# Index lists of a graph network's gathers without a bound

## The chip, the cores and the metric

The kernel runs on one core of a Trainium2 chip. The metric is device time in microseconds (us), the median of several executions; a profile of one execution goes with it. In the profile PE is TensorE, PEld its weight load, DVE is VectorE, ACT is ScalarE, POOL is GpSimd, SP is the engine that issues plain transfers.

## The reference

Two layers of a relational graph attention network, a residual and a layer norm, on N = 3125 nodes with 768 features, E = 53,125 edges sorted by destination, and R = 3 relations. The first layer has 4 heads of 192, the second 1 head of 768.

```
def rgat_conv(x, W, q, k, b, src, dst, etype, heads, out_ch, n_nodes):
    xr = einsum('nd,rdf->rnf', x, W)          # a row for each node and relation
    oi = xr[etype, dst]; oj = xr[etype, src]
    alpha = leaky_relu(oi @ q + oj @ k, 0.2)
    m = segment_max(alpha, dst);  e = exp(alpha - m[dst])
    z = segment_sum(e, dst);      a = e / (z[dst] + 1e-16)
    msg = a[:, :, None] * oj.reshape(-1, heads, out_ch)
    return segment_sum(msg, dst) + b

h = elu(rgat_conv(x, W1, q1, k1, b1, ...))
out = layernorm(x + rgat_conv(h, W2, q2, k2, b2, ...))
```

## The kernel before

The nodes are taken in 25 groups (NB) of up to 128. The edges of a group are laid over 17 slots of 128 lanes (SL; 14 in group 0), a lane for an edge. Slots are whole, so some of their lanes hold edges of the next group, or, in the last group, lie behind the last edge. These lanes have a place `dl` in the group of 128 or more and never match a node.

For each slot the kernel gathers rows by an index list (`ridx`, 3 x source + relation), 128 indices for one instruction on POOL: `gather_rows`, L485. It does so from three tables in HBM of 9600 rows each (25 x 128 x 3; the rows of real nodes end at 3125 x 3 = 9375): `kt1`, the key products of layer 1, 16 bytes a row; `tab1`, the transformed rows of layer 1, 3088 bytes; `tab2`, those of layer 2, 3088 bytes. There are 24 x 17 + 14 = 422 slots, so 3 x 422 = 1266 gathers, all from the one line L490, and the profile tells them apart by their target: `kt`, `share` and `g` (tab1), `G` (tab2).

The stages follow each other in an order that is written out by hand (a list of steps for each count of products or gathers), with no reordering behind it:

- **0 to about 108 us**: preparation of the edges, key and query products.
- **Phase 1**, to about 770 us. For each group an index chain: a transpose into PSUM (`a_index`), then `a_index2` (L575) on DVE, which makes `dl` (L580), the index list, `rel` (L588) and a limit `lim` (L592); `a_next` and `a_next2` find where the next group begins. With the list there, the group's kt gathers are issued (for groups 0 to 20), and scores, a segmented maximum by scan and weights `pall` are made. Meanwhile TensorE makes the rows of tab1 from x (L742); every sixth of its matmuls waits for a gather that lies 8 earlier, as "an even load".
- **Loading of the second weights**, to about 820 us.
- **Phase 2**, to about 1756 us. The tab1 gathers go into 14 buffers (9 `share` and 5 `g`); per group the weighted sums are matmuls in two batches (L1028, 8 and 9 slots), and between these lie the matmuls of the second layer's rows (L1121). A gather waits for the sums of the slot 14 before. The kt gathers of the last four groups lie between, four to a group (`KEYS`), for groups 2 to 18.
- **Phase 3**, to the end. The tab2 gathers go into 44 buffers, with scores, scan, sums (L1340), layer norm and output beside them.

A gather of the kernel before carries a bound, 9599: a lane whose index is above it isn't transferred. `a_index2` adds 2^20 to the index of every lane outside its group (L584, L585), so that those lanes are dropped. A dropped lane leaves in its buffer what was there, so for groups 0 to 2, where a buffer has no rows yet, the index is limited to 9599 instead (`rfirst`, L587).

Of the kernel before, what the change touches and what calls it, by code (L numbers as in the profile page):

```python
# [8 lines left out]
F32 = mybir.dt.float32  # L9
# [3 lines left out]
I32 = mybir.dt.int32  # L13
AF = mybir.ActivationFunctionType
ALU = mybir.AluOpType
# [5 lines left out]
P = 128  # L21
# [11 lines left out]
def _index(ap):  # L33
    return bass.IndirectOffsetOnAxis(ap=ap, axis=0)
# [3 lines left out]
SL = 17  # L38
# [22 lines left out]
def kernel(  # L61
# [20 lines left out]
    N, D = x.shape  # L82
    R = layers[0]["W"].shape[0]
    E = src.shape[0]
    NB = (N + P - 1) // P
    NP = NB * P
# [11 lines left out]
    LL = FRONT + E + BACK  # L98
    NK = (NB - 1) * SL + SLF
    V, S, G, T = nc.vector, nc.scalar, nc.gpsimd, nc.tensor  # L100
    OOB = float(1 << 20)

    dram = ctx.enter_context(tc.tile_pool(name="fdram", bufs=1, space=DRAM))
    keep = ctx.enter_context(tc.tile_pool(name="keep", bufs=1))
    first_rows = {0: 0, 1: 1, 2: 2}

    ed_d = dram.tile([4, LL], F32, name="ed_d")
    dr_d = dram.tile([1, LL], BF, name="dr_d")
# [30 lines left out]
    oidx = keep.tile([P, 1], I32, name="oidx")  # L139
    flag = keep.tile([1, 1], I32, name="flag")  # L140
    ridx = keep.tile([P, NB, SL], I32, name="ridx")
    rfirst = keep.tile([P, len(first_rows), SL], I32, name="rfirst")
    dl = keep.tile([P, NB, SL + 1], F32, name="fdl")
    rel = keep.tile([P, NB, SL], F32, name="rel")
    pall = keep.tile([P, NB, SL, H1], F32, name="pall")
# [318 lines left out]
    def slots(b):  # L464
        return SL if b else SLF
# [18 lines left out]

    def gather_rows(to, tab, b, j):  # L485

        i = ridx[:, b]
        if b in first_rows:
            i = rfirst[:, first_rows[b]]
        return G.indirect_dma_start(out=to, out_offset=None, in_=tab, in_offset=_index(i[:, j:j + 1]),  # L490
                                    bounds_check=NP * R - 1, oob_is_err=False)

    def start(b, into):

# [56 lines left out]
    def phase1(pre, work, psum, wH, wL, qq):  # L551
# [23 lines left out]
        def a_index2(b):  # L575
            pT = st[b]["pi"]
            c = SL + 1

            p3 = pT[:SHIFT, :3 * c].rearrange("p (r k) -> p r k", r=3)
            V.tensor_copy(p3[:, :, 0], p3[:, :, slots(b)])  # L580
            V.tensor_scalar(dl[:, b, :], pT[:, c:2 * c], 1.0 / BIG, n_all[:, b:b + 1], op0=ALU.mult,
                            op1=ALU.subtract)
            inv = work.tile([P, SL], F32, name="inv", bufs=2)
            V.tensor_scalar(inv, dl[:, b, :SL], float(P), OOB, op0=ALU.is_ge, op1=ALU.mult)  # L584
            V.tensor_add(ridx[:, b, :], pT[:, 0:SL], inv)  # L585
            if b in first_rows:
                V.tensor_scalar(rfirst[:, first_rows[b], :], ridx[:, b, :], NP * R - 1, None, op0=ALU.min)  # L587
            V.tensor_copy(rel[:, b, :], pT[:, 2 * c:2 * c + SL])  # L588

            s = st[b]  # L590
            s["lim"] = work.tile([P, 1], F32, name="lim", bufs=2)
            V.tensor_scalar(s["lim"], n_all[:, b:b + 1], float(P), float(N), op0=ALU.add, op1=ALU.min)  # L592
# [39 lines left out]
        def a_gather(b, j):  # L632
            gathered[b, j] = gather_rows(kts[b % 3][:, j, :], kt1, b, j).ins
# [180 lines left out]
        for _ in range(4):  # L814
            T.matmul(ahead[0][:, :P], ident, ident, start=True, stop=True)
        d_split(1)
        a_index2(0)
        for j in range(SLF):
            a_gather(0, j)
# [28 lines left out]
        ev = {}  # L848

        chain = ((-6, a_index), (-6, a_index2), (-5, a_gathers), (-5, a_next), (-4, a_next2))  # L850
        turn = [base(b) * STEPS // NE for b in range(NB - LATE)]
        for b, n in enumerate((4, 3, 2, 1)):
# [39 lines left out]
        for n in range(max(ev) + 1):  # L892
            for f, b in ev.get(n, ()):
                f(b)
            b, i = divmod(n, 6)
# [37 lines left out]
    def phase2(work, psum, wH, wL):  # L933
# [19 lines left out]
        def key(b, j):  # L953
            gather_rows(kts[b % 2][:, j, :], kt1, b, j)
# [43 lines left out]
        def gather(k):  # L998
            gather_rows(gs[k % NG], tab1, *in_turn(k))
# [545 lines left out]
    with tc.manual_schedule():  # L1545
        with tc.tile_pool(name="share", bufs=1) as pool:
# [4 lines left out]
            with tc.tile_pool(name="wbuf", bufs=1) as wbuf:  # L1551
                wH = wbuf.tile([P, DT, WW], F32R, name="wH")
                wL = wbuf.tile([P, DT, WW], F32R, name="wL")
                with tc.tile_pool(name="pre", bufs=1) as pre:
                    qq = pre.tile([P, NB, H1, R], F32, name="qq")
                    with tc.tile_pool(name="work0", bufs=1) as work, tc.tile_pool(
                        name="psum0", bufs=1, space=PSUM
# [23 lines left out]
                    with tc.tile_pool(name="work1", bufs=1) as work, tc.tile_pool(  # L1581
                        name="psum1", bufs=1, space=PSUM
# [544 lines left out]
```

## Time and profile before

| what | us |
|---|---|
| runs | 2512.51, 2497.31, 2531.09 |
| median | 2512.51 |
| profiled execution | 2528.77 |
| its span | 2527.0 |
| PE busy | 1899.4 (75%) |
| POOL busy | 1332.5 (53%) |
| DVE busy | 1199.7 (47%) |
| mean granted clock of TensorE | 0.839 |
| bytes moved, all queues | 506.39 MB |

The span is that of the profiled execution, a little longer than the median run. "Busy" counts instructions at work. A row of instructions names line, engine, operation, output<-inputs, and in square brackets the idle time before it with what ended it. A windows row gives for a stretch of the span the busy time of each engine, the granted clock, the share of the DMA engines and GB/s.

### The profile page before, as it was taken

Reading aid. Unit: us, or ns where it says so; the run is one execution under the profiler, and the core shown is the slowest. Engines: PE = TensorE matmul, PEld = TensorE weight load, DVE = VectorE, ACT = ScalarE, POOL = GpSimd, SP = SyncE. Lnnn points to the kernel's source line nnn. Section 1 sums busy time; section 2 is a strip of 40 time slices with the busy share of each in tenths; the row PEclk is TensorE's granted clock in tenths of the full one; section 3 lists DMA queues with packets and bytes.
Section 4 is the critical chain, followed back from the end, with each engine's and each line's share of the span. In section 5 each row is a group of like instructions: output and inputs, shape, how many; then the busy total and the mean of one; then the engine's idle time right before and its main releaser. Section 6 shows DMA issues by size and latency. Waiting matters only on the chain.

```text
span 2527.0 us, 40133 instructions
## 1 busy us (share of the span) xinstructions
PE 1899.4 (75%) x13939; PEld 1335.0 (53%) x13939; DVE 1199.7 (47%) x4331; ACT 383.1 (15%) x834; POOL 1332.5 (53%) x1326
## 2 busy tenths in 40 slices
PE   8958987787689688889889889997445444465556
PEld 8746766576568466666666667766122222222223
DVE  7424434333344564555555656652254444445445
ACT  6301111111111011111111111111011111111111
POOL 4355666554350565555555565551656555556552
PEclk9978989898889789899999999999566666676667
DMA  7533444343338766666666768874777777777772
GB/s 228 146 112 112 150 146 149 102 144 113 119 110 307 248 214 206 212 197 211 217 202 213 223 206 253 252 229 169 254 237 269 256 265 239 236 239 246 239 243 102
DMA packets 161765, 506.39 MB, mean 200 GB/s; under 512 B 48027, under 2 KB 57520, under 8 KB 161555
## 3 DMA queue, kind: packets, MB, share of 16 engines
q0 software_dynamic: 81936, 331.52, 42.5%
q1 hardware_dynamic: 69389, 157.78, 17.8%
q10 hardware_dynamic: 10230, 14.43, 1.7%
q8 instruction: 114, 1.87, 0.3%
q14 instruction: 96, 0.79, 0.1%
HBM read 412.74 MB, written 95.69 MB: 201 GB/s over the span
## 4 chain that ended last, share of the span: by engine, by line
PE 51%; issue 20%; another core or an unknown queue 9%; POOL 8%; DVE 7%; DMA 2%; ACT 1%; POOLq 0%; DVEq 0%; SPq 0%; ACTq 0%
PE po L1121 17%; PE po L742 16%; PE acc L1028 9%; POOL G L490 7%; PE acc L1340 3%; DVE selp L482 2%; PE bank L299 1%; DMA G<-ftab,ridx 1%; PE pt L277 1%; PE pt L1095 1%; PE po L414 1%; PE px L714 1%; DVE sT L1251 0%; PE pq L649 0%
## 5 line engine op out<-in xcount | busy, mean ns | idle before, releaser
L490 POOL DMA_INDIRECT kt<-kt,ridx x374 | 393.8, 1053 | 260.6 <-DVE al L672 111.9
L490 POOL DMA_INDIRECT G<-ftab,ridx x374 | 378.2, 1011 | 273.4 <-PE acc L1340 118.2
L1121 PE MATMUL po<-wH,hT 128*128 128x512 f32 (+1 forms) x1500 | 449.9, 384 | 32.4 <-ACT r L1148 17.2
L742 PE MATMUL po<-wH,xT 128*128 128x512 f32 (+1 forms) x1320 | 431.6, 403 | 46.5 <-issue 34.3
L1340 PE MATMUL acc<-G,selp 128*32 128x384 f32 (+1 forms) x2292 | 303.8, 635 | 162.6 <-issue 88.9
L482 DVE TENSOR_SCALAR selp<-frow,fdl,pall 128x32 f32<-128x32 f32 (+1 forms) x1688 | 380.6, 316 | 31.7 <-remote 26.4
L490 POOL DMA_INDIRECT share<-ftab,ridx x239 | 239.9, 1004 | 206.1 <-PE acc L1028 125.4
L1121 PEld LDWEIGHTS po<-wH,hT 128*128 128x128 f32 x1500 | 274.4, 192 | 107.6 <-issue 37.4
L742 PEld LDWEIGHTS po<-wH,xT 128*128 128x128 f32 x1320 | 258.1, 204 | 103.4 <-issue 46.1
L1340 PEld LDWEIGHTS acc<-G,selp 128*32 128x32 f32 x2292 | 127.6, 133 | 312.5 <-issue 191.7
L1121 PE MATMUL po<-wL,hT 128*128 128x512 f32 (+1 forms) x750 | 285.4, 381 | 0.5 <-issue 0.2
L742 PE MATMUL po<-wL,xT 128*128 128x512 f32 (+1 forms) x660 | 261.2, 396 | 11.2 <-issue 10.1
L1028 PE MATMUL acc<-share,selp 128*32 128x193 f32 x3088 | 229.5, 363 | 46.0 <-issue 35.2
L490 POOL DMA_INDIRECT g<-ftab,ridx x135 | 136.0, 1007 | 129.0 <-PE acc L1028 79.5
L1028 PEld LDWEIGHTS acc<-share,selp 128*32 128x32 f32 x3088 | 144.0, 120 | 109.2 <-issue 87.3
L1148 ACT COPY r<-po 128x262 f32<-128x262 f32 (+5 forms) x175 | 71.2, 436 | 713.5 <-PE po L1121 348.4
L1121 PEld LDWEIGHTS po<-wL,hT 128*128 128x128 f32 x750 | 144.4, 193 | 28.4 <-issue 2.0
L742 PEld LDWEIGHTS po<-wL,xT 128*128 128x128 f32 x660 | 134.3, 203 | 39.3 <-issue 16.5
L1028 PE MATMUL acc<-g,selp 128*32 128x193 f32 x1688 | 134.3, 350 | 15.8 <-issue 15.1
L1251 DVE TENSOR_SCALAR sT<-bc,cols 128x512 bf16<-128x512 f32 (+1 forms) x125 | 82.8, 662 | 96.2 <-PE bc L1245 93.2
L1245 PE MATMUL bc<-d,one 1*128 1x512 bf16 (+1 forms) x125 | 48.8, 391 | 96.3 <-DVE sT L1251 65.1
L1028 PEld LDWEIGHTS acc<-g,selp 128*32 128x32 f32 x1688 | 82.6, 116 | 48.5 <-issue 38.6
(309 smaller groups left out, 1963.7 us busy)
## 6 DMA issues: line engine op xcount, KB each, us to landing
ftab<-r SPq DMA_DIRECT2D x74, 386.0 KB
ftab<-share SPq DMA_DIRECT2D x71, 386.0 KB
share<-in_L_gnn_W_dram SPq DMA_DIRECT2D x36, 384.0 KB
w_d<-w2hl SPq DMA_DIRECT2D x18, 768.0 KB
sT<-dr_d SPq DMA_DIRECT2D x25, 534.0 KB
share<-in_x_dram SPq DMA_DIRECT2D x27, 384.0 KB
xb_d<-share SPq DMA_DIRECT2D x25, 384.0 KB
xr<-in_x_dram SPq DMA_DIRECT2D x21, 384.0 KB
```

Of the source, the lines that this page charges most:

```text
L277: T.transpose(pt[:, f, c * P:(c + 1) * P], a[:, (2 * i + f) * P:(2 * i + f + 1) * P], ident)
L299: T.matmul(to, a[:, 2 * i + f, :], t[:, f, :w], start=(n == 0), stop=(n == 2 * DT - 1))
L414: T.matmul(po[g][:, :HALF], a[:, t % 2, :], w[:, t, KQ + r * D + c * HALF:][:, :HALF], start=(t == 0 and n == 0), stop=(t == DT - 1 and n ...
L482: V.tensor_scalar(sel.rearrange("p (t f) -> p t f", f=32), of, dl[:, b, j:j + 1], p, op0=ALU.is_equal, op1=ALU.mult)
L490: return G.indirect_dma_start(out=to, out_offset=None, in_=tab, in_offset=_index(i[:, j:j + 1]), bounds_check=NP * R - 1, oob_is_err=False)
L742: m = T.matmul(po[:, :n], xT[:, s, t, :], w[:, t, KQ + f:KQ + f + n], start=(i == 0), stop=(i == 3 * DT - 1))
L1028: T.matmul(acc[32 * t:32 * t + 32, h // 2, c], sel[:, h, 32 * WINDOW[i].index(t):][:, :32], g[:, h * CW:(h + 1) * CW], start=(i == u[0] an ...
L1121: T.matmul(po[:, :n], hT[:, k, t, :], w[:, t, f:f + n], start=(i == 0), stop=(i == 3 * DT - 1))
L1148: S.copy(o[:, 1 + at - a:1 + at + m], po[:, got - a:got + m])
L1245: T.matmul(bc[:, :n], one, s["d"][:, 4 * i * P:4 * i * P + n], start=True, stop=True)
L1251: V.tensor_scalar(s["sT"][:, 4 * i * P:4 * i * P + n], bc[:, :n], cols[:, b:b + 1], None, op0=ALU.is_equal)
L1340: T.matmul(acc[32 * t:32 * t + 32, c, :HALF + c], st[b, j][:, 32 * WINDOW[j].index(t):][:, :32], gs[:, (base(b) + j) % NG, 1 + c * HALF:][ ...
```

## The change

`gather_rows` passes neither a bound nor the flag that goes with it, and always takes `ridx`. `a_index2` doesn't mark the lanes outside their group any more: the index that stands at the lane, which is that of its own edge (of the next group) is limited to 0 and the last real row, 9374, in one instruction. With this every lane of every gather transfers a row. The marked sum, the first groups' own list and its tile go.

```diff
-    OOB = float(1 << 20)
-    first_rows = {0: 0, 1: 1, 2: 2}
...
-    rfirst = keep.tile([P, len(first_rows), SL], I32, name="rfirst")
...
     def gather_rows(to, tab, b, j):
 
-        i = ridx[:, b]
-        if b in first_rows:
-            i = rfirst[:, first_rows[b]]
-        return G.indirect_dma_start(out=to, out_offset=None, in_=tab, in_offset=_index(i[:, j:j + 1]),
-                                    bounds_check=NP * R - 1, oob_is_err=False)
+        return G.indirect_dma_start(out=to, out_offset=None, in_=tab, in_offset=_index(ridx[:, b, j:j + 1]))
...
-            inv = work.tile([P, SL], F32, name="inv", bufs=2)
-            V.tensor_scalar(inv, dl[:, b, :SL], float(P), OOB, op0=ALU.is_ge, op1=ALU.mult)
-            V.tensor_add(ridx[:, b, :], pT[:, 0:SL], inv)
-            if b in first_rows:
-                V.tensor_scalar(rfirst[:, first_rows[b], :], ridx[:, b, :], NP * R - 1, None, op0=ALU.min)
+            V.tensor_scalar(ridx[:, b, :], pT[:, 0:SL], 0.0, float(N * R - 1), op0=ALU.max, op1=ALU.min)
```

## The prediction

> **What bounds the kernel now.** I read the shares and the chain of the page first, then the windows stage by stage, then who waits for whom in each stage, and last the gathers themselves, since they are what the change touches.
>
> ```profile
> span 2527.0 us, 40133 instructions
> PE 1899.4 (75%) x13939; PEld 1335.0 (53%) x13939; DVE 1199.7 (47%) x4331; ACT 383.1 (15%) x834; POOL 1332.5 (53%) x1326
> PE 51%; issue 20%; another core or an unknown queue 9%; POOL 8%; DVE 7%; DMA 2%; ACT 1%; POOLq 0%; DVEq 0%; SPq 0%; ACTq 0%
> ```
>
> The chain that ended last is TensorE for half of the span. POOL, which issues the 1266 gathers, carries 8% of it. So a gather is not the pace of the kernel as a whole; what it is worth depends on the stage.
>
> ```profile
> 820.00:1000.00 180.00, 140.63 (x1190) 103.42 (x1194) 96.27 (x421) 16.09 (x33) 99.83 (x99) 0.84 0.71 226
> 1000.00:1250.00 250.00, 219.92 (x1910) 161.11 (x1906) 134.45 (x570) 29.62 (x60) 140.62 (x139) 0.93 0.66 207
> 1250.00:1490.00 240.00, 215.12 (x1885) 163.29 (x1881) 135.25 (x580) 28.60 (x60) 134.67 (x134) 0.93 0.69 215
> 1490.00:1755.00 265.00, 250.80 (x2254) 189.09 (x2243) 144.98 (x622) 37.77 (x79) 118.45 (x118) 1.00 0.70 222
> 1756.00:1815.00 59.00, 18.19 (x79) 5.46 (x79) 16.70 (x81) 1.59 (x2) 42.27 (x42) 0.53 0.85 287
> 1815.00:2485.00 670.00, 356.82 (x2747) 149.40 (x2746) 304.23 (x964) 88.20 (x111) 384.16 (x381) 0.66 0.73 244
> ```
>
> After the stretch's length the columns are the busy time of TensorE, its weight load, VectorE, ScalarE and POOL, then the granted clock, the DMA share and GB/s. The first four rows are phase 2, and its last one is close to a TensorE bound: 251 of 265 us busy at clock 1.00. The rows before it are not, and the waits name the difference:
>
> ```profile
> PE po L742 <- issue: 45.2, 52, 4.5
> PE acc L1028 <- issue: 44.8, 97, 1.1
> PE acc L1028 <- issue: 5.5, 21, 1.0
> PE acc L1340 <- issue: 88.9, 45, 7.4
> POOL kt L490 <- DVE al L672: 111.9, 9, 24.0
> POOL G L490 <- PE acc L1340: 129.4, 23, 8.7
> ```
>
> These are, in order, TensorE in phase 1 (110 to 760 us), in phase 2 before 1490, in phase 2 after 1490, and in phase 3, with the total, the times and the longest; then what POOL itself waited for in phases 1 and 3. In phase 1 POOL waits for VectorE to free a buffer, in phase 3 for TensorE to finish with one of 44: there the gathers run ahead. "issue" is a wait for nothing that the profile shows. Before 1490 the late 16-byte gathers (kt) lie among the others, four to a group; after it there are none, and the wait falls from 44.8 to 5.5 us. One such place, POOL first and TensorE below it:
>
> ```profile
> 1206.20 1.00 POOL L490 DMA_INDIRECT kt<-kt,ridx  x1 [0.30 <-issue]
> 1207.50 1.00 POOL L490 DMA_INDIRECT kt<-kt,ridx  x1 [0.30 <-issue]
> 1208.81 1.00 POOL L490 DMA_INDIRECT kt<-kt,ridx  x1 [0.30 <-issue]
> 1210.11 1.00 POOL L490 DMA_INDIRECT kt<-kt,ridx  x1 [0.30 <-issue]
> ...
> 1209.56 0.49 PE L1028 MATMUL acc<-share,selp 128*32 128x193 f32 x2 [0.94 <-issue]
> 1210.97 0.49 PE L1028 MATMUL acc<-share,selp 128*32 128x193 f32 x2 [0.92 <-issue]
> 1212.40 0.38 PE L1028 MATMUL acc<-g,selp 128*32 128x193 f32 x2 [0.95 <-issue]
> ```
>
> The sums step forward in pauses of 0.9 us while the four kt gathers are under way, and run freely behind them. I don't know what holds them; I take the pauses to last as long as the gathers do. A gather costs POOL 1.00 us and 0.30 us of "issue": a period of 1.30 us.
>
> **The change, part by part.**
>
> *The gather without a bound.* No row of this trace shows one. What there is:
>
> ```profile
> L490 POOLq MOVE  x1266: 29/29/29, 90.5 to 2480.0; - x181
> L490 POOL DMA_INDIRECT kt<-kt,ridx x374: 993/1000/1749, 190.7 to 1506.6; - x187
> L490 POOL DMA_INDIRECT kt<-kt,rfirst x48: 993/1000/1608, 108.3 to 186.2; - x48
> 68.47 0.73 POOL L397 DMA_DIRECT2D kt<-kk  x1 [3.18 <-DVE kk L396]
> 69.22 0.38 POOL L400 TENSOR_TENSOR qq<-g 128x12 f32<-128x12 f32 x2
> 2483.04 1.00 POOL L490 DMA_INDIRECT G<-ftab,ridx  x1 [0.30 <-issue]
> 2484.34 1.00 POOL L490 DMA_INDIRECT G<-ftab,ridx  x1 [0.30 <-issue]
> ```
>
> (Minimum, median and maximum in ns in the first three.) The 1266 moves that put the bound into a register go, 29 ns each. They lie on POOL's queue beside the gather before, so I cost them at nothing; without that cover it is 37 us over the run, 0.03 per gather. The check's own price can't be read off: gathers whose indices were clamped (rfirst) take 1.00 us, and so do the last two of all, whose every lane is past the bound. The work doesn't depend on the outcome of the check, which doesn't say that the check is free. From below, a plain DMA of 128 partitions, with no list and no bound, takes 0.73 us and the next instruction follows it with no pause: 0.57 under the period. From above, the slowest gather took 1.75 us: 0.75 over it. The nearest row is the gather with its bound. What it has and the plain one lacks is the pause of 0.30, which a list of indices, or an operand from a register, may cause; I take half of it, a saving of **0.15 us** (11.5% of 1.30), and keep both ends.
>
> What that is worth, stage by stage: the pauses of TensorE under kt gathers are 45.2 + 44.8 = 90 us, and 11.5% of them is 10.4. In phase 3 the 88.9 us lie partly in the first fill of 44 buffers, where the DMA share is 0.85 and the transfers set the landing, and for the rest in groups that POOL runs ahead of; I count half, 11.5% of 44 = 5.1. Elsewhere a quicker gather meets the buffers that POOL waits for already (the rows of 111.9 and 129.4) and waits longer: 0.
>
> *The index arithmetic.*
>
> ```profile
> L584 DVE TENSOR_SCALAR inv<-fdl x25: 176/177/178, 106.8 to 797.5; 128x17 f32<-128x17 f32 x25
> L585 DVE TENSOR_TENSOR ridx<-pT,inv x25: 175/176/178, 107.0 to 797.7; 128x17 int32<-128x17 f32 x25
> L587 DVE TENSOR_SCALAR rfirst<-ridx x3: 174/176/239, 107.2 to 163.9; 128x17 int32<-128x17 int32 x3
> POOL kt L490 <- DVE lim L592: 32.5, 5, 15.7
> ```
>
> 50 instructions of 0.18 become 25 of the same kind and shape, and the three minima go: 28 x 0.18 = 5.0 us of VectorE, which is 47% busy. On the path are only the places where POOL waits for the index list, five in phase 1 by the last row (it names the next instruction, lim): 5 x 0.18 = 0.9 us, say 1. Nothing else moves: on every engine the order of what stays is as before, SP's queue included, and no wait is added.
>
> *The rows that were skipped.* By the inputs, 768 of 54,016 lanes per table lie outside their group and past the clamped first groups; 370 of them are the end of the last group.
>
> ```profile
> DMA packets 161765, 506.39 MB, mean 200 GB/s; under 512 B 48027, under 2 KB 57520, under 8 KB 161555
> q0 software_dynamic: 81936, 331.52, 42.5%
> ```
>
> Now each fetches its row: 768 x 3088 bytes x 2 tables = 4.74 MB, 0.9% of 506.39 (the third table's rows have 16 bytes). At the 222 and 244 GB/s of the windows this is 2.37/0.222 + 2.37/0.244 = 20 us of transfer, but at a DMA share of 0.70 and 0.73, beside TensorE in phase 2 and 44 buffers in phase 3; that hides it, and I charge nothing. Without the cover it is the 20 us, half of it in the last group, where the last three gathers of each table become whole ones and the 370 lanes all read the last row.
>
> *Sum.* 10.4 + 5.1 + 1 = 16.5 us, so the profiled execution of 2528.77 us (span 2527.0) would be 2512. That execution is 16 us above the median of the three runs, 2512.51, from which I forecast **2496 us**, 0.7% less.
>
> **The rivals.**
>
> *A far cheaper gather that frees TensorE too.* The check and its register are the main part of what sets a gather apart, and it drops to the plain DMA's 0.73 us, 44% less. 44% of the 90 us is 40, of the 44 in phase 3 19. Then the clock: where pauses are rare (the window from 1490) 1.00 is granted, before it 0.84 and 0.93. At 1.00 the 576 us of TensorE there would be shorter by at most 9% (the mean before 1490 is 0.91), 54 us; half of it is 27. With the 1 us of indices this is 87: **2426 us**, and some 2450 with half of the clock's part. For it: the step from 44.8 to 5.5 us between neighbouring windows. Against: the list of 128 indices stays. The Trainium skill (TensorE: Matmul & The Clock Gate, Part 1) says that the clock falls to half after an idle window of about 3.4 us and is full again after a busy one; the windows agree in direction, and by that rule the clock's part comes all or nothing as pauses fall under one window.
>
> *The change does nothing to a gather.* Its time is that of making 128 descriptors, which stay 128. For it: the same 1.00 us for lists of every kind. Then only the 1 us of indices is left: **2511 us**. The Trainium skill (DMA: Bandwidth & Descriptors, the latency section) puts about 1 us on the emission of a DMA by the GpSimd path, whatever it moves, and names no bound; the trace's 1.00 us agrees, and by that rule the gather would stay as it is.
>
> *Slower: a gather without a bound takes POOL longer, and POOL becomes the pace.* A bound lets the lane be dropped; without one, another path of the same engine might be walked.
>
> ```profile
> L490 POOL DMA_INDIRECT G<-ftab,ridx x374: 994/1002/1429, 1834.1 to 2484.3; - x187
> ```
>
> In phase 3, 374 gathers take 650 us, 29.6 us for a group of 17. POOL's 17 x 1.30 = 22.1 fit in; from a period of 1.74 us they don't. A gather as slow as this row's slowest, 1.43 + 0.30 = 1.73, stands at that point: the pauses of 90 us grow by a third, +30, and phase 1, with bursts of 17, loses some 10 at its start. At 1.85 phase 3 adds 22 groups x 1.9 = 42. So +40 to +85, about **2575 us**. Against: no reason in the trace why less work should take longer.
>
> **How the numbers follow.** My forecast (saving 0 to 0.3 us per gather, 2480 to 2508) has 0.38; the far cheaper gather 0.30 (2400 to 2465); no effect 0.11 (2505 to 2520); slower 0.21 (2540 to 2610). The range, 2420 to 2585, leaves out a third of the cheap gather and nearly half of the slow one, 0.2 together; it takes in the 20 us of uncovered transfer. Two per cent, 50 us, is about what a measurement of this kernel can tell from no change: its three runs lie 34 us apart. Faster by more than that (under 2462): nearly all of the cheap gather and a little of mine, 0.31. Slower (over 2563): most of the last case, 0.19. Within: 0.50.
>
> **What would show it.** In the profile after, the gather's median and the pause before it in a burst: 0.85 to 1.0 us and 0.15 to 0.3 for my case. The rows "acc L1028 <- issue" and "po L742 <- issue" should lose about a tenth; if they fall by far more, or the clock before 1490 reaches 1.00, the first rival holds. Bytes of q0 rise by 4.7 MB, and no move stands before a gather. I am wrong if the pauses don't follow the gather's length at all (they may be made by the small rows, which stay), if the last group ends late behind its 370 equal rows, or if the gather's time leaves 0.7 to 1.3 us.

## The result, and the profile after

The changed kernel takes **2637.48 us** (median of 4 runs, 2622.75 to 2651.93) against 2521.8 for the kernel before: ratio **1.051**, 95% interval 1.044 to 1.057. It is slower, where 0.7% less was forecast. Five series of runs followed, each with its own runs of the kernel before on the same chip, and they fell into two kinds: in three of them the kernel before took 2512 to 2528 us again, in two it took 1944 and 1946. The results give no reason for the two kinds. The comparison above belongs to the first kind, which the text calls *held*; the second is called *free*. What separates them in the profile is the subject of this section and the next.

From the page of the changed kernel in the held series above: span, busy shares, packets, and the engines' shares of the chain that ended last.

```profile
span 2650.1 us, 38839 instructions
PE 1899.9 (72%) x13939; PEld 1344.5 (51%) x13939; DVE 1191.9 (45%) x4303; ACT 382.8 (14%) x834; POOL 1257.2 (47%) x1326
DMA packets 161755, 511.06 MB, mean 193 GB/s; under 512 B 47263, under 2 KB 56756, under 8 KB 161555
PE 33%; issue 17%; another core or an unknown queue 11%; POOL 11%; DVE 2%; DMA 2%; ACT 2%; SPq 0%; POOLq 0%; DVEq 0%; ACTq 0%
```

TensorE has the same work (1899.9 us against 1899.4) and VectorE and POOL have less. 4.67 MB more are moved. All the same the span is 123 us longer, so the time went into waiting. The gathers did get cheaper; by the view of their line in the changed kernel (L484; minimum, median and maximum in ns, then the first and last start):

```profile
L484 POOL DMA_INDIRECT kt<-kt,ridx x422: 938/944/1717, 107.7 to 1581.2; - x141
L484 POOL DMA_INDIRECT G<-ftab,ridx x422: 940/946/1380, 1837.6 to 2607.3; - x141
L484 POOL DMA_INDIRECT share<-ftab,ridx x272: 940/946/1258, 874.6 to 1783.1; - x136
```

0.946 us against 1.002, and with the pause of 0.30 a period (from the start of one gather to the start of the next) of 1.25 against 1.306. No move is left. The first starts date the loss: the first gather of tab1 stood at 825.1 and is now at 874.6 (+49.5 us in phase 1), the first of tab2 at 1760.2 and now 1837.6 (+27.9 in phase 2), and the remaining 45.7 us are phase 3. There it is spread over the groups: from one `oh` to the next, most groups take longer than before, by up to 6.6 us, and some are up to 3 us shorter. In a later held series the same changed kernel had its first tab1 gather at 869.3 and its first tab2 gather at 1796.6 us, in a span of 2611.0. So the loss of phases 1 and 3 came again (44 and 48 us), and that of phase 2 did not (927.3 us against 935.1 before).

The waits over the whole run, the kernel before first (VectorE, then TensorE) and the changed one below (its lines have other numbers: L1260 is L1271 of before, L1329 is L1340, L1017 is L1028, L731 is L742, L479 is L482):

```profile
DVE oh L1271 <- remote: 208.8, 24, 29.4
PE acc L1340 <- DVE selp L482: 66.7, 12, 8.9
PE acc L1028 <- issue: 50.3, 118, 1.1
```

```profile
DVE oh L1260 <- remote: 259.8, 24, 19.5
PE acc L1329 <- DVE selp L479: 185.2, 23, 9.1
PE acc L1017 <- issue: 66.2, 127, 1.6
PE po L731 <- issue: 57.7, 58, 3.0
```

The waits of TensorE for L742 stood in the prediction: 45.2 us. Every group of phase 3 but one has the wait in the first row. "remote" is the profile's word for a wait whose end it can put down to no instruction. The product `oh` on VectorE needs 17 small matmuls of TensorE (`pq`), and in the program it waits for nothing else on another engine. One group of the changed kernel, TensorE, VectorE and POOL from the timeline:

```profile
2007.55 0.62 PE L1254 MATMUL pq<-q2s,sT 128*128 128x9 bf16 x17
...
2018.95 0.32 DVE L1260 TENSOR_TENSOR oh<-oh,pq 128x153 f32<-128x153 f32 x1 [10.30 <-remote]
...
2016.32 0.95 POOL L484 DMA_INDIRECT G<-ftab,ridx  x1 [0.30 <-issue]
2017.58 0.95 POOL L484 DMA_INDIRECT G<-ftab,ridx  x1 [0.30 <-issue]
2021.42 0.94 POOL L484 DMA_INDIRECT G<-ftab,ridx  x1 [2.90 <-remote]
```

By the profile the 17 matmuls start within 0.62 us from 2007.55 on, and 16 matmuls of the sums follow them. Yet VectorE starts `oh` at 2018.95, when POOL's unbroken row of gathers has just ended. Counted from the start of the last of the 17 to the start of `oh`, the median of the 25 groups is 11.4 us here, 8.6 in the kernel before, and 0.57 in a free series; in the last group, with no gather left, it is 0.56 here too. While VectorE stands, the `selp` that it makes behind `oh` isn't there, and TensorE waits in turn: that is the second row. The profile models the ends of matmuls, so it can't say whether the work or the word of it is late.

The same is seen at the start of phase 1. These are the windows view, 108 to 130 and 130 to 150 us, for the kernel before and the changed one (columns as in the prediction: TensorE and its count first, the clock, the DMA share and GB/s last), and then single starts in the changed kernel: a matmul of the index chain and the instruction on VectorE that needs it, and a row of TensorE's products:

```profile
108.00:130.00 22.00, 18.22 (x88) 14.60 (x87) 6.05 (x23) 2.07 (x8) 16.75 (x17) 1.00 0.83 166
130.00:150.00 20.00, 2.61 (x8) 1.71 (x7) 0.00 (x0) 0.80 (x1) 14.39 (x15) 0.63 0.07 2
```

```profile
108.00:130.00 22.00, 19.40 (x87) 15.42 (x85) 5.14 (x21) 2.08 (x8) 16.82 (x18) 0.92 0.72 165
130.00:150.00 20.00, 3.16 (x9) 2.38 (x9) 0.00 (x0) 0.80 (x1) 12.54 (x14) 0.56 0.04 1
```

```profile
126.86 0.28 PE L587 MATMUL pT<-fdl,after 128*128 128x1 f32 x2
151.50 0.28 DVE L590 TENSOR_SCALAR n_all<-pT,n_all,lim 128x1 f32<-128x1 f32 x1 [27.46 <-remote]
...
133.90 0.37 PE L731 MATMUL po<-wH,xT 128*128 128x256 f32 x1 [1.83 <-issue]
136.00 0.37 PE L731 MATMUL po<-wH,xT 128*128 128x256 f32 x1 [1.73 <-issue]
137.40 0.37 PE L731 MATMUL po<-wL,xT 128*128 128x256 f32 x1 [1.03 <-issue]
140.20 0.38 PE L731 MATMUL po<-wH,xT 128*128 128x256 f32 x1 [2.42 <-issue]
143.00 0.37 PE L731 MATMUL po<-wH,xT 128*128 128x256 f32 x1 [2.42 <-issue]
```

VectorE starts 24.6 us after the matmul that it needs. Of TensorE's matmuls, eight or nine start in 20 us, and the starts shown lie 2.1, 1.4, 2.8 and 2.8 us apart: multiples of 0.70. This is the **hold**: beside a row of gathers TensorE makes one step at a time, or the word of its results comes late.

The hold doesn't set in with the first gather of a row. POOL's row began at about 108 us, and through its first 17 or 18 gathers, at the same period, TensorE nearly kept its pace (88 and 87 matmuls in 22 us); only behind them did it stop. Nor does the hold grow with the number of gathers under way. Counted from the DMA packets of the changed kernel's trace, 4 to 5 gathers were under way at each start from the 7th to the 16th, and 2 in the held part behind.

### The profile page after: what moved, and what is told of

It reads as the page before. It is cut to its first block, busy times and chain, and to the rows that moved or that the text cites. A ratio compares the mean times of both kernels' runs of the same rounds, so it can differ in the third digit from the quotient of the medians.

```text
span 2650.1 us, 38839 instructions
## 1 busy us (share of the span) xinstructions
PE 1899.9 (72%) x13939; PEld 1344.5 (51%) x13939; DVE 1191.9 (45%) x4303; ACT 382.8 (14%) x834; POOL 1257.2 (47%) x1326
## 4 chain that ended last, share of the span: by engine, by line
PE 33%; issue 17%; another core or an unknown queue 11%; POOL 11%; DVE 2%; DMA 2%; ACT 2%; SPq 0%; POOLq 0%; DVEq 0%; ACTq 0%
PE po L1110 15%; POOL G L484 11%; PE acc L1017 8%; PE po L731 6%; PE acc L1329 2%; DMA G<-ftab,ridx 1%; ACT r L1137 1%; PE pt L1084 0%; ACT ey L1036 0%; PE acc L1373 0%; ACT hT L1091 0%; DVE sT L1240 0%; DVE selp L479 0%; DMA ftab<-r 0%
## 5 line engine op out<-in xcount | busy, mean ns | idle before, releaser
L484 POOL DMA_INDIRECT G<-ftab,ridx x422 | 400.5, 949 | 423.7 <-PE acc L1329 170.3
L484 POOL DMA_INDIRECT kt<-kt,ridx x422 | 417.9, 990 | 379.4 <-DVE al L661 140.1
L731 PE MATMUL po<-wH,xT 128*128 128x512 f32 (+1 forms) x1320 | 437.6, 407 | 77.9 <-ACT share L763 39.3
L1110 PE MATMUL po<-wH,hT 128*128 128x512 f32 (+1 forms) x1500 | 457.9, 388 | 44.7 <-ACT r L1137 33.2
L1329 PE MATMUL acc<-G,selp 128*32 128x384 f32 (+1 forms) x2292 | 293.5, 639 | 210.7 <-DVE selp L479 185.2
L484 POOL DMA_INDIRECT share<-ftab,ridx x272 | 257.8, 948 | 354.9 <-PE acc L1017 185.7
L479 DVE TENSOR_SCALAR selp<-frow,fdl,pall 128x32 f32<-128x32 f32 (+1 forms) x1688 | 380.5, 325 | 26.1 <-remote 20.3
L731 PEld LDWEIGHTS po<-wH,xT 128*128 128x128 f32 x1320 | 261.8, 207 | 140.1 <-issue 50.6
L1329 PEld LDWEIGHTS acc<-G,selp 128*32 128x32 f32 x2292 | 131.7, 136 | 346.2 <-DVE selp L479 217.4
L731 PE MATMUL po<-wL,xT 128*128 128x512 f32 (+1 forms) x660 | 263.1, 399 | 21.0 <-issue 20.8
L1017 PE MATMUL acc<-share,selp 128*32 128x193 f32 x3088 | 220.8, 356 | 52.3 <-issue 42.6
L484 POOL DMA_INDIRECT g<-ftab,ridx x150 | 142.8, 952 | 139.8 <-PE acc L1017 82.5
L1017 PEld LDWEIGHTS acc<-share,selp 128*32 128x32 f32 x3088 | 139.0, 118 | 114.6 <-issue 92.9
L731 PEld LDWEIGHTS po<-wL,xT 128*128 128x128 f32 x660 | 136.3, 207 | 46.3 <-issue 23.5
L1017 PE MATMUL acc<-g,selp 128*32 128x193 f32 x1688 | 136.0, 354 | 23.8 <-issue 23.6
L1260 DVE TENSOR_TENSOR oh<-oh,pq 128x153 f32<-128x153 f32 x25 | 7.9, 316 | 259.8 <-remote 259.8
```

Of the source, the lines that this page charges most:

```text
L479: V.tensor_scalar(sel.rearrange("p (t f) -> p t f", f=32), of, dl[:, b, j:j + 1], p, op0=ALU.is_equal, op1=ALU.mult)
L731: m = T.matmul(po[:, :n], xT[:, s, t, :], w[:, t, KQ + f:KQ + f + n], start=(i == 0), stop=(i == 3 * DT - 1))
L1017: T.matmul(acc[32 * t:32 * t + 32, h // 2, c], sel[:, h, 32 * WINDOW[i].index(t):][:, :32], g[:, h * CW:(h + 1) * CW], start=(i == u[0] an ...
L1110: T.matmul(po[:, :n], hT[:, k, t, :], w[:, t, f:f + n], start=(i == 0), stop=(i == 3 * DT - 1))
L1260: V.tensor_mul(oh, oh, s["pq"][:, :SL * R * 3].rearrange("p (j k) -> p j k", j=SL))
L1329: T.matmul(acc[32 * t:32 * t + 32, c, :HALF + c], st[b, j][:, 32 * WINDOW[j].index(t):][:, :32], gs[:, (base(b) + j) % NG, 1 + c * HALF:][ ...
```

## The experiments

The theories at first: the missing bound makes the loss, by the period of the gathers or by the unbounded form itself; or the rows that were skipped make it. Each run is given with its ratio to the kernel before in its own series. None of the kernels leaves out a part of the computation.

### The bound given back (held series)

```diff
-    return G.indirect_dma_start(..., in_offset=_index(ridx[:, b, j:j + 1]))
+    return G.indirect_dma_start(..., in_offset=_index(ridx[:, b, j:j + 1]),
+                                bounds_check=NP * R - 1, oob_is_err=False)
```

> The changed kernel with the bound of 9599 given to every gather again; its indices stay limited to 0 and 9374, so no lane is dropped and every row moves. If the missing bound itself makes the loss (by whatever way), this comes back to the kernel before, 2505 to 2530 us, with a gather of 1.00 us and a period of 1.305. If the 768 rows per table that were skipped before make it, it stays at 2620 to 2650.

Measured: 2514.99 us, ratio 0.9965 (0.992 to 1.001). The whole loss is gone, though every lane still moves its row and the shorter index arithmetic stays. So the 768 rows per table cost nothing that can be seen, and the missing bound is the cause. With the bound two things come back, the longer gather (0.998 us in this run) and the move before it; the section on the moves takes them apart.

### The bound for phase 3 alone (held series)

```diff
+    bound = dict(bounds_check=NP * R - 1, oob_is_err=False) if tab is tab2 else {}
```

> The changed kernel with the bound given back to the gathers of phase 3 alone. If each stage pays for its own unbounded gathers, the 42 us of phase 3 come back and the rest stays: 2585 to 2605 us. If the loss of phase 3 is a consequence of something earlier, it stays at 2620 to 2650.

Measured: 2578.11 us, ratio 1.019 (1.008 to 1.029). This is a little under the range expected. Phase 3 takes 766.3 us in its profile, as before (766.8), and phase 1 keeps its loss (first tab1 gather at 877.1). So these two stages pay for their own unbounded gathers. Phase 2 took 934.4 us, as before, with unbounded gathers: its loss in the first profile is not shown to belong to them.

### A tiny work on POOL before each gather (held series)

`pad` is one float; in the first run the memset stands in the changed kernel, in the second in the kernel before.

```diff
+    G.memset(pad, 0.0)
     return G.indirect_dma_start(...)
```

> The changed kernel with one tiny GpSimd memset before each gather, so that unbounded gathers stand farther apart. If the loss comes from the closer spacing of the gathers (1.25 us against 1.305), a spacing back at 1.3 us or more gives most of it back: 2500 to 2560 us, and the waits of VectorE for oh fall from 11.4 us to 6 to 9. If it comes from the unbounded form as such, whatever its spacing, it stays at 2620 to 2670.

> The kernel before with the same tiny memset before each gather. If the spacing between gathers is what decides how far TensorE is held, this becomes faster than the kernel before, 2440 to 2500 us. If POOL's time is all that counts, it costs nothing or up to 40 us: 2515 to 2560.

Measured: 2646.77 us (ratio 1.047, 1.039 to 1.056) and 2571.63 us (1.018, 1.010 to 1.026). The first lies in the range that stood for the unbounded form as such, the second in neither of its ranges. The timeline says why the first can't decide: the memset goes into the pause, and the distance of the gathers stays as it was.

```profile
2000.28 0.95 POOL L486 DMA_INDIRECT G<-ftab,ridx  x1 [0.22 <-issue]
2001.22 0.09 POOL L485 MEMSET pad<- 1x1 f32 x1
2001.53 0.97 POOL L486 DMA_INDIRECT G<-ftab,ridx  x1 [0.22 <-issue]
```

1.25 us as without it. In the kernel before, too, the period stays (1.305), and yet the memset costs 1.8%; why is open.

### Gathers farther apart (held series)

First the changed kernel with each gather waiting for the landing of the one three before (POOL idle in between), then with four memsets (POOL busy in between), then the kernel before with the wait.

```diff
+    apart = mybir.DependencyInfo(mybir.DependencyClass.Sync, mybir.DependencyReason.DATA)
+    g = G.indirect_dma_start(...)
+    if len(sent) >= 3:
+        tc.add_manual_dep(g.ins, sent[-3], apart, reason="apart")
+    sent.append(g.ins.name)
```

```diff
+    for _ in range(4):
+        G.memset(pad, 0.0)
```

> The changed kernel, each gather waiting for the landing of the gather three before, so that at most three are under way; a landing takes 4.5 us, so the period in a burst grows from 1.25 to some 1.5 us, and the added time is idle on POOL. If TensorE is held because gathers follow each other without a long enough pause, this is faster than the changed kernel, 2480 to 2580 us, and VectorE's waits for oh shrink. If only POOL's own pace counts, it is as slow or slower: 2640 to 2720.

> The changed kernel with four tiny memsets on POOL before each gather, some 0.36 us of work: the period grows to about 1.5 us as in the run with three gathers under way, but POOL is busy in it. If the distance between two gathers decides, this is faster than the changed kernel as that run is, 2480 to 2580 us. If an idle POOL decides, it is not: 2640 to 2720.

> The kernel before, bound included, with the same wait for the gather three before. If idle pauses on POOL let TensorE through, this is faster than the kernel before: 2430 to 2490 us. If the bound does another thing, it gains nothing: 2510 to 2570.

Measured: 2502.14 us (0.994, 0.988 to 1.001), 2595.71 (1.036, 1.028 to 1.044) and 2460.56 (0.980, 0.969 to 0.990). With the wait, both kernels are faster than without it. With the four memsets the gain is small: 1.036 against 1.051 and 1.045 for the changed kernel in its own two held series, with intervals that touch; its time lies between the two ranges expected. What the waits for `oh` are left with (the view of its line; us and times), in the changed kernel with the wait and with the four memsets:

```profile
  PE pq L1261: 8.0, 10
  remote: 3.4, 3
```

```profile
  PE pq L1257: 1.3, 3
```

From 260 us to 11 and to 1. At the start of phase 1, the run with the memsets:

```profile
130.00:150.00 20.00, 20.00 (x133) 16.74 (x132) 11.34 (x38) 3.96 (x13) 16.03 (x56) 1.00 0.61 189
```

133 matmuls where there were 9, at full clock, with POOL gathering all the time. This window alone would not do: with one memset, at 1.25 us, it has 94 matmuls, because POOL's row was broken there by a pause of 3.1 us, and the hold came later, at about 147 us. The whole run does: with four memsets no "issue" row of TensorE is above 4.6 us. With the wait, 44.1 us remain at the products of phase 1 and 34.3 at the sums of phase 2.

So gathers that lie farther apart free TensorE, with or without a bound, and neither an idle POOL nor the check is needed for it. Closeness is not the whole condition: the first gathers of a row don't hold TensorE, and in the free series below none do, with more gathers under way (4.3 on the mean in phase 3 against 3.6 held, by the packets). With four memsets the period is 1.63 us, and 2.09 for most gathers of phase 2. POOL then becomes the bound: the gathers of tab1 take 1030 us in place of 881 to 909. That is why that run as a whole gains little.

### The moves (held series, then free, then held)

The bound taken from one register that is set once, so without the 1266 moves: first in the changed kernel, then in the kernel before, the latter in a series of each kind.

```diff
+    if not once:
+        once.append(G.to_reg(NP * R - 1))
-    ... bounds_check=NP * R - 1, oob_is_err=False)
+    ... bounds_check=once[0], oob_is_err=False)
```

> The changed kernel with a bound of 9599 on every gather, taken from one register that is set once: the gather checks its bound, but no move stands before it. If the check in the gather is what helps, this is like the kernel before: 2500 to 2530 us. If the move before each gather (29 ns on POOL's queue) is what helps, this stays like the changed kernel: 2620 to 2650.

> The kernel before, skipped rows and all, with its bound taken from one register set once, so without the 1266 moves. If the moves cost (as the run with one register against the one with the bound given back says, some 25 to 40 us), this is 2460 to 2500 us. If the index arithmetic made that difference, it stays at 2505 to 2530.

> The kernel before with its bound in one register, so without the 1266 moves. Where the kernel before takes 1944 us this is the same (0.9998 measured). Where it takes 2510: 2460 to 2500 us if the moves are what the run with the bound in one register saved there, 2505 to 2530 if it was something else.

Measured: 2473.6 us (0.986, 0.977 to 0.995); 1942.96 in the free series (0.9998, 0.9988 to 1.0007); 2474.92 in the held one (0.982, 0.973 to 0.990). The first lies below both of its ranges: the changed kernel loses nothing once its gathers check a bound, without any move. So it is the check, with the 0.05 us that it adds to the gather, that gave the loss back, and the move is a cost of its own. The second had its ranges from a held chip. The moves cost 1.8% where TensorE is held and nothing where it isn't, at almost the same period (1.305 with them, 1.302 without). They take 29 ns each on POOL's queue, 37 us in all, and the loss is 53: so they seem to act on the hold, in a way that the runs don't show.

The free series was not planned. This is what the kernel before without moves (the same time as the kernel before there) shows in it: from the page, span and busy shares, then the windows view of 130 to 150 us:

```profile
span 1940.2 us, 38868 instructions
...
PE 1670.7 (86%) x13939; PEld 1250.9 (64%) x13939; DVE 1202.2 (62%) x4331; ACT 382.5 (20%) x834; POOL 1333.6 (69%) x1326
```

```profile
130.00:150.00 20.00, 20.00 (x128) 16.44 (x127) 11.56 (x39) 3.31 (x11) 15.43 (x16) 1.00 0.66 209
```

But for the moves the same instructions, the same gathers 1.30 us apart, and no hold: the wait for `oh` isn't in its list at all. The two kinds lie some 570 us apart. That the hold makes all of it is the nearest reading; the next experiment bears on it.

### Two memsets, and the distance by stages

The changed kernel with two memsets before each gather, in a free and a held series:

```diff
+    for _ in range(2):
+        G.memset(pad, 0.0)
```

> The changed kernel with two tiny memsets on POOL before each gather: by the run with four (period 1.63 us) the period becomes about 1.33 us, a little over that of a gather with its bound, without the bound. If the period alone decides how far TensorE is held, this is near the kernel before: 2500 to 2560 us. If it is the check in the gather, or an idle POOL, it stays at 2600 to 2660.

> The changed kernel with two tiny memsets on POOL before each gather, a period of 1.33 us without a bound. Where the kernel before takes 1944 us this is 2225 again. Where it takes 2510: 2500 to 2560 us if the period decides how far TensorE is held, 2600 to 2660 if the check in the gather or an idle POOL does.

Measured: 2225.02 us in the free series (1.144, 1.142 to 1.146) and **2385.7 us in the held one (0.949, 0.940 to 0.959)**, the fastest of all there, 9% under the changed kernel of the same series (2635.93). Both numbers expected for a held chip were too high, since the period isn't 1.33 throughout. A gather that also waits for a semaphore starts later behind a memset; from phase 2 of the held run:

```profile
1205.41 0.23 POOL L486 MEMSET pad<- 1x1 f32 x2
1206.27 0.94 POOL L487 DMA_INDIRECT share<-ftab,ridx  x1 [0.62 <-issue]
1207.21 0.23 POOL L486 MEMSET pad<- 1x1 f32 x2
1208.07 0.94 POOL L487 DMA_INDIRECT share<-ftab,ridx  x1 [0.62 <-issue]
```

1.80 us here and in most of phase 2, 1.33 for most of the others. Where TensorE is held, a step of 1.8 us now and then lets it through (waits for `oh` 36 us in all); where it isn't, the added time of POOL is simply lost.

By the first starts of the gathers, this kernel's phases 2 and 3 take nearly the same in both kinds: 916.8 us held against 918.4 free, and 681.0 against 667.5. Only phase 1 is far longer, 781.4 against 636.5. For the kernel before, all three are longer in a held series, by 190 to 201 us each (the free one without moves). So with the spacing most of the difference between the kinds goes, which speaks for the hold as its cause, though a stage at POOL's pace could hide another.

The same held series tells the distance from the unbounded form. The first tab1 gather starts at 869.3 us in the changed kernel (1.25 us, no bound), at 807.2 in the kernel before without moves (1.30, bound), and at 781.4 with the two memsets (1.33, no bound): the order is that of the distance. At 130 to 150 us, in a pure row of 1.33, TensorE is held all the same (28 matmuls in 20 us). So between 1.33 us, where the hold is still there, and 1.63, where it is gone, lies a point that no run narrowed down.

Two kernels with the distance in some stages only came to the free series, and cost there as more time of POOL does. In both the bound comes from one register: the wait for the gather three before on the kt gathers alone, then with a wait for the gather four before on the two large tables as well.

> The bound from one register on every gather, and the wait for the gather three before on the kt gathers alone. The run with three under way took 16 us less than the one with one register in phase 1 and 16 and 37 us more in phases 2 and 3. If these stages add up, this takes 2440 to 2465 us, below both kernels. If the gain in phase 1 is lost again behind it, 2465 to 2485.

> As the run before, and the gathers of both large tables waiting for the gather four before. A landing takes 4.6 us, four under way allow a period of 1.15 to 1.4 us, so POOL is held back little. If a short idle pause now and then frees TensorE, the waits of VectorE for oh fall from 7.9 us to 1 to 4 and the time to 2400 to 2450. If nothing short of three under way helps, it is 2450 to 2480.

Measured: 2046.72 us (1.053, 1.051 to 1.055) and 2149.34 (1.104, 1.100 to 1.108). Written for a held chip, these expectations can't be judged. A third, the two memsets in phases 1 and 3 with a bounded phase 2, came to a free series too:

> The changed kernel with the two memsets before the gathers of phases 1 and 3 alone; those of phase 2 have the bound from one register and no memset. Where TensorE is held, phase 2 took 870 us with the two memsets and 862 to 866 with the register, so 2375 to 2390 us if the stages add up. Where the kernel before takes 1944 us, phase 2 had 869 us with the memsets and 681 without, so some 2030 us.

Measured: 2043.61 us (1.050, 1.049 to 1.052); the second number stood close, and whether it holds where TensorE is held was not seen.

### The change itself, once more in each kind of series

> The changed kernel itself, beside the kernel before. On a chip where the kernel before takes about 2510 us (TensorE held in the bursts of gathers) it is 5% slower again, 2620 to 2650 us. On one where the kernel before takes 1944 us the stages go at POOL's pace, and a gather that is 0.055 us shorter then gives time back: 1266 times 0.055 is 70 us at most, and for the stages that are at POOL's pace 30 to 60: 1885 to 1915 us. If an unbounded gather is bad by itself, it is over 1950 there too.

> The changed kernel beside the kernel before once more. Where the kernel before takes about 2510 us: 2610 to 2650 again. Where it takes 1944 us, with TensorE not held: 1885 to 1915 if a gather that is 0.055 us shorter gives its time back there, over 1950 if an unbounded gather is bad by itself.

Measured: 2635.93 us in a held series (1.045, 1.037 to 1.054), as expected, and **1923.66 us in a free one, ratio 0.989 (0.987 to 0.991): faster by 22 us**, where 30 to 60 were expected. The gathers of tab2 in the free series, without moves but with the bound first, then the changed kernel, and the windows view of the latter from 700 to 1300 us, in phase 2:

```profile
L494 POOL DMA_INDIRECT G<-ftab,ridx x374: 994/998/1297, 1426.8 to 1913.9; - x187
L494 POOL DMA_INDIRECT G<-ftab,rfirst x48: 994/998/1357, 1363.6 to 1425.5; - x48
```

```profile
L484 POOL DMA_INDIRECT G<-ftab,ridx x422: 942/946/1391, 1362.4 to 1892.0; - x141
```

```profile
700.00:1300.00 600.00, 600.00 (x6114) 475.97 (x6105) 431.29 (x1854) 94.79 (x196) 408.96 (x429) 1.00 0.84 284
```

1363.6 to 1913.9 is 550.3 us, 1362.4 to 1892.0 is 529.6: 421 distances of 1.307 and 1.258 us, POOL's own pace. The 20.7 us between them are nearly all of the gain. Phases 1 and 2 have none (tab1 starts at 629.3 and 630.4); the window shows why, TensorE busy for 600 of 600 us.

## Why the prediction was wrong

**The gather.** That a gather without a bound is cheaper was right. The saving was taken as 0.15 us, half of the pause, and is 0.055; it lies in the gather (1.002 to 0.946), and the pause of 0.30 stays. So the term was sized almost three times too large.

**What the saving is worth** is the step that failed: "I take the pauses to last as long as the gathers do". 11.5% of 90 us was to come off TensorE's pauses in phases 1 and 2, and 11.5% of half of the 88.9 in phase 3. These terms, 15.5 of the 16.5 us, had the wrong sign. The prediction itself named the doubt ("the pauses don't follow the gather's length at all") and gave it no price. The pauses were rightly found, but they don't shrink with the gather: with gathers 4% closer they grew, 50.3 to 66.2 us at the sums of phase 2 and 45.2 to 57.7 at the products of phase 1 (64.0 and 56.9 in the later held series). In phase 3 the row that the prediction priced, 88.9 us, fell to 24.1, but the wait for `selp` beside it rose from 66.7 to 185.2, and both stand behind VectorE's wait for `oh`, which rose from 208.8 to 259.8. Setting the gathers 1.63 us apart made these waits vanish. The record shows that closer gathers make the waits longer; by what way they hold TensorE stays open. The 0.00 us of VectorE between 130 and 150 us, beside 15 gathers and next to no DMA, stood in the trace of before; read then, it would have said that something other than bandwidth or POOL's time stops the engines there.

**The moves** were costed at nothing because POOL's queue hides them. In a free series that is so (0.9998); in a held one they cost 1.8%, more than the 37 us named for an uncovered queue. Their going is part of the change. Against the kernel before without moves, in the same series, the changed kernel loses 161 us (2635.93 against 2474.92).

**The skipped rows** (nothing, up to 20 us uncovered) and **the index arithmetic** (1 us) are not contradicted: with both changed and the bound back, the time is that of before within 0.8%. The runs can't resolve 1 us.

**The rivals.** The slower one had the right sign and the wrong mechanism: gathers did not get longer, POOL did not become the pace, and its share of busy time fell from 53 to 47%. That a gather doesn't change at all fell too, though by little: 1.002 to 0.946 us. The far cheaper gather, at 0.73 us, did not come either; of its argument only this stands, that the clock is low where TensorE pauses: 0.839 before, 0.824 after, 0.915 and 0.917 in the free series, 0.56 and 0.63 in the windows of the hold. By the rule of the Trainium skill (TensorE: Matmul & The Clock Gate, Part 1) idle windows halve the clock; these numbers agree. The text reads the low clock as an effect of the hold and not as its cause; no run tested it.

**Where TensorE is not held**, the change goes the way of the forecast and comes near its size (0.7% forecast, 1.1% measured), but by luck: the forecast had 10.4 us from phases 1 and 2 and 5.1 from phase 3, and measured were none and 20.7. Phase 3 runs at POOL's pace there, and the 0.05 us of each of its gathers comes off the end.

## What to carry to other kernels

An engine that is not the bound can still slow another by how closely its instructions follow each other, so a cheaper instruction in a burst is not free of risk; a pause that the profile puts down to "issue" should be tested by moving the bursts apart before a saving is scaled with it. Where an engine stands still beside a burst of gathers, look for the smallest spacing that frees it and weigh it against the stages that run at POOL's pace: two tiny memsets were worth 5% in one kind of series and cost 14% in the other. Measure such a change in more than one series, with the kernel before beside it each time.

## What was not expected of the hardware

- Rows of gathers 1.25 to 1.31 us apart held TensorE in three of five later series and in the first, after some 17 gathers in the first row. Beside 16-byte rows its instructions started on a grid of 0.70 us; beside 3088-byte rows VectorE started 11.4 us (median) after the matmuls that it needs, and 0.57 where nothing was held. At 1.63 us it was gone. What makes the hold, and why two series did not have it, stays open; moving the other queues' transfers or TensorE's own waits was not tried.
- A bound on a gather costs POOL about 0.05 us (0.946 to 1.002 held, 0.946 to 0.998 free).
- A lane past the bound saves POOL nothing: all-skipped gathers take the same 1.00 us, and 4.7 MB more of rows did not show in the time.
- 1266 moves of 29 ns that run beside the gathers cost 1.8% where TensorE was held, and nothing where it was not.
